# Local-attention stack: scores over four row groups into four PSUM banks shared with the outputs, and a new step order

## The chip, the core and the metric

The kernel runs on one core of a Trainium2 chip as one program. The metric is device time in microseconds (us), the median of several executions. One execution was also taken with the hardware profiler; its trace gives start and duration of every instruction on the five engines: TensorE (PE, with its weight loads as PEld), VectorE (DVE), ScalarE (ACT), GpSimd (POOL) and SyncE (SP, which here only issues DMAs).

## The reference, cut to what matters

The input is 16 sequences of 256 tokens with 128 features, in float32. A first part applies one small attention block, one mixture-of-experts block and one retention block. After it comes the stack that the change is about, six layers deep:

```python
for i in range(DEPTH):                                   # DEPTH = 6
    x = attn_layer(shift_tokens(x), ...) + x             # 16 heads of 64, window 32
    x = ffn_layer(shift_tokens(x), ...) + x

# attn_layer, per sequence and head:
q, k = rotary(l2norm(q) * qs), rotary(l2norm(k) * ksc)   # rotary with position-dependent scale
sim  = einsum("bhwie,bhwje->bhwij", q_windows, k_two_windows) * 8   # 32 queries against 64 keys
out  = einsum("bhwij,bhwje->bhwie", softmax(where(mask, -max, sim)), v_two_windows)
return out @ Wo

# ffn_layer: LayerNorm, x @ W1 + b1, a * gelu(gate), @ W2 + b2   (inner width 341)
```

So in the stack each window of 32 queries sees 64 keys: its own window and the one before. All arithmetic is float32.

## The kernel before, in words

**Units.** The stack is cut into 96 units: one sequence in one layer (`Unit`, 6 layers of 16). Two sequences share a feed-forward (`Forward`, 48 of them). A unit is a list of small steps, each a method that issues a few instructions on one engine:

- `pqk.G.k` (PE, four matmul instructions of 128x256) projects queries (k=0) or keys (k=1) of head group G into one of two PSUM banks. Four heads of a group lie on the four groups of 32 partitions. `sq` (ACT) squares the result, `t2` and `rot` (DVE) multiply it with the rotary tables, `add.G` (POOL) adds the two. The PSUM bank is free when `sq`, `t2` and `rot` are done.
- `nr.0` and `nr.1` (PE) sum the squares per head, `rnA`, `rnB`, `rnC` (DVE, ACT, DVE) make the reciprocal norm, `bcD` (SP) writes it to DRAM and reads it back spread over partitions (one DMA `ndr<-rn`, then eight `bc<-ndr`), and `norm.G` (POOL) multiplies it in.
- `s` (PE) computes scores. A float32 matmul is two weight loads and two matmul instructions; one `s` step holds 32 matmuls of 32x32 weights against 64 columns, so 64 matmul instructions. There are eight `s` steps in a unit. `sm` (DVE) adds the mask while it copies the scores out of PSUM; `mx`, `sub`, `exp`, `su`, `rec`, `nm` (DVE, POOL, ACT, DVE, DVE, DVE) make the softmax.
- `pv.i` (PE) projects the values, `vc.i` (ACT) copies them to SBUF, and `vs.0`, `vs.1` (SP, four DMAs `v<-v` each) make a copy that is shifted by one window.
- `pt`, `pTc` (PE, ACT) transpose the probabilities, `o.hu.tt` (PE, 64 matmul instructions, four steps in a unit) computes outputs, which read both copies of the values; `oTc` (ACT) copies them out of PSUM, `y.0`, `y.1` and `xsu` (PE, PE, DVE) project and add to x.
- A feed-forward is `fn`, `nat`, `st`, `rs`, `z`, `trf`, `fz` (LayerNorm with two transposes), then `fg`, `gl`, `fa`, `fh` three times, `fy` and `xsf`.

**PSUM.** Eight banks: two for `pqk`, two that all small results (`misc`) take in turn, two for scores (`ps_sc`) and two for outputs (`ps_ob`). A score tile is [128, 2, 512], for half the row groups (`hu` = 0 or 1), and an output tile is [128, 2, 512] for half the tokens (`tt`); each of the two pools has one buffer, so tiles of a pool follow each other in it.

**Order.** Nothing is scheduled at run time or by the framework: every engine executes its instructions in the order in which the steps are written. That order is the string `ORDER` (215 words, one iteration handles two units). In iteration j a word such as `s.0.0.1:2` calls step `s(0, 0, 1)` of unit 2j+2, `fy:-4` that of unit 2j-4; iterations overlap, so one iteration works on units that are up to nine apart. `:2` in one iteration is `:0` in the next. `BRIDGE` is the same for the passage from the first part. SP too takes its DMAs in this order: one that has to wait holds up those behind it. Weights of the next layer are issued by `follow` when the last unit has used the old ones.

Of the kernel before, what the change touches and what calls it, by code (L numbers as in the profile page):

```python
# [15 lines left out]
P = 128  # L16
# [94 lines left out]
def kernel(ctx: ExitStack, tc: tile.TileContext, a: dict, widths: dict, out: bass.AP):  # L111
# [742 lines left out]
    ps_o = ctx.enter_context(tc.tile_pool(name="ps_ob", bufs=1, **psum))  # L854
# [35 lines left out]
    def load_ff(l):  # L890
        w1 = kc.tile([P, 2 * FF], F32, tag="w1", name=f"w1_{l}")
        w2 = kc.tile([P, 3, D], F32, tag="w2", name=f"w2_{l}")
        nc.sync.dma_start(out=w1, in_=a["w1"][l])
        nc.sync.dma_start(out=w2[:, 0:2, :], in_=a["w2"][l, 0:256].rearrange("(c p) n -> p c n", p=P))
        nc.sync.dma_start(out=w2[0 : FF - 256, 2, :], in_=a["w2"][l, 256:FF])
        return w1, w2
# [3 lines left out]
    class Unit:  # L900
# [118 lines left out]
        def p_s(self, hu):  # L1019
            return self.tile(ps_s, [P, 2, 2, 2, 2, 2 * WIN], "s", hu, tag="s")  # L1020

        def s(self, hu, tt, gh):
            ps, qk = self.p_s(hu), self.qk_t
            for G in (2 * gh, 2 * gh + 1):
                for hf in range(2):
                    for b in range(4):
                        for r2 in range(2):
                            rows = slice(32 * (2 * hu + r2), 32 * (2 * hu + r2) + 32)
                            at = WIN * (4 * tt + b)
                            keys = qk[G][rows, 1, hf, at : at + 2 * WIN]  # L1030
                            if b % 2 == 0:
                                keys = keys.rearrange("f (n t) -> f n t", n=2)[:, ::-1, :]
                            nc.tensor.matmul(  # L1033
                                ps[32 * b : 32 * b + 32, r2, tt, G // 2, G % 2, :],
                                lhsT=qk[G][rows, 0, hf, WIN + at : 2 * WIN + at],
                                rhs=keys,
                                start=(hf == 0),
                                stop=(hf == 1),
                            )
# [8 lines left out]
        def sm(self, hu):  # L1048
            nc.vector.tensor_tensor(  # L1049
                self.t_sm(hu).rearrange("n r t g p c -> n r (t g p c)"),  # L1050
                self.p_s(hu).rearrange("n r t g p c -> n r (t g p c)"),
# [40 lines left out]
        def t_pT(self, hu, tt):  # L1092
            return self.tile(s3, [P, 512], "pT", hu, tt, bufs=3)
# [5 lines left out]
        def p_o(self, tt):  # L1099
            return self.tile(ps_o, [P, 2, 4, P], "o", tt, tag="o")  # L1100
# [349 lines left out]
```

## Time and profile before

| | |
|---|---|
| median of 3 executions | 4274.9 us (4269.47 to 4275.85) |
| profiled execution, its own time | 4277.4 us |
| its span, first to last instruction | 4275.7 us |
| mean granted TensorE clock | 0.969 of full speed |
| PE busy | 4036.9 us (94%) |
| DVE busy | 2940.5 us (69%) |
| POOL busy | 2527.3 us (59%) |
| ACT busy | 2077.0 us (49%) |

A line of the trace names the source line, engine, operation, tiles (out<-in), shape, count and time. L1033 is the matmul of `s`, L1111 that of `o`, L921 `pqk`, L955 `nr`, L1015 the DMAs of `vs`, L980 and L986 those of `bcD`, L1239 `fy`. In "idle before" or in the waits, the name behind the arrow is what the engine waited for. A busy PE is not PE at its peak: ends of matmuls are modelled, and a wait can hide under the last matmul's modelled end.

### The profile page before, as it was taken

Reading aid. Unit: us, or ns where it says so; the run is one execution under the profiler, and the core shown is the slowest. Engines: PE = TensorE matmul, PEld = TensorE weight load, DVE = VectorE, ACT = ScalarE, POOL = GpSimd, SP = SyncE. Lnnn points to the kernel's source line nnn. Section 1 sums busy time; section 2 is a strip of 40 time slices with the busy share of each in tenths; the row PEclk is TensorE's granted clock in tenths of the full one; section 3 lists DMA queues with packets and bytes.
Section 4 is the critical chain, followed back from the end, with each engine's and each line's share of the span. In section 5 each row is a group of like instructions: output and inputs, shape, how many; then the busy total and the mean of one; then the engine's idle time right before and its main releaser. Section 6 shows DMA issues by size and latency. Waiting matters only on the chain.

```text
span 4275.7 us, 216376 instructions
## 1 busy us (share of the span) xinstructions
PE 4036.9 (94%) x100320; PEld 2776.4 (65%) x100320; DVE 2940.5 (69%) x5436; ACT 2077.0 (49%) x3344; POOL 2527.3 (59%) x1419
## 2 busy tenths in 40 slices
PE   6999978999999999999999999999999999999998
PEld 4666655666666666666666666666666666666664
DVE  4677646677777677667777766767677777667774
ACT  2555534455554445444554544545445544545453
POOL 2454556666665666656666665666556666656661
PEclk8999988999999999999999999999999999999999
DMA  3111112222222222222222222122232212222231
GB/s 98 44 41 48 36 40 67 69 60 65 70 58 53 69 65 60 70 64 57 65 58 70 60 68 71 48 63 64 65 72 57 68 44 71 63 69 67 48 74 44
DMA packets 209187, 260.84 MB, mean 61 GB/s; under 512 B 54174, under 2 KB 164892, under 8 KB 207388
## 3 DMA queue, kind: packets, MB, share of 16 engines
q1 hardware_dynamic: 207852, 246.74, 23.2%
q8 instruction: 786, 12.88, 1.3%
q14 instruction: 117, 0.96, 0.1%
q10 hardware_dynamic: 432, 0.26, 0.0%
HBM read 140.98 MB, written 17.83 MB: 37 GB/s over the span
## 4 chain that ended last, share of the span: by engine, by line
PE 68%; DMA 9%; DVE 8%; POOL 6%; ACT 4%; issue 3%; SPq 3%; POOLq 0%; ACTq 0%; DVEq 0%
PE pqk L921 13%; PE s L1033 10%; PE o L1111 9%; PE pv L999 7%; DMA v<-v 6%; PE y L1130 5%; PE nr L955 4%; PE fy L1239 3%; PE pt L1088 3%; POOL qk L993 3%; PE fg L1209 2%; PE fa L1222 2%; PE p L330 2%; DVE sm L1082 1%; SPq L986 1%
## 5 line engine op out<-in xcount | busy, mean ns | idle before, releaser
L946 POOL TENSOR_TENSOR qk<-qk,t 128x1024 f32<-128x1024 f32 x384 | 906.6, 2363 | 282.1 <-DVE qk L940 276.0
L993 POOL TENSOR_TENSOR qk<-qk,bc 128x1024 f32<-128x1024 f32 x384 | 947.4, 2484 | 79.9 <-DMA v<-v 73.0
L1064 POOL TENSOR_TENSOR sm<-sm,mx 128x1024 f32<-128x1024 f32 x192 | 365.9, 1906 | 991.0 <-DVE mx L1060 274.3
L921 PE MATMUL pqk<-xs,wqk 128*128 128x256 f32 x3072 | 852.9, 406 | 20.0 <-ACT sq L929 9.6
L1033 PEld LDWEIGHTS s<-qk 32*32 32x32 f32 x49152 | 536.6, 104 | 393.6 <-issue 376.3
L929 ACT ACTIVATE sq<-pqk 128x512 f32<-128x512 f32 x768 | 454.2, 599 | 665.1 <-DVE qk L940 355.5
L940 DVE TENSOR_TENSOR qk<-pqk,rot 128x512 f32<-128x512 f32 x768 | 515.1, 681 | 308.4 <-PE pqk L921 249.2
L935 DVE TENSOR_TENSOR t<-pqk,rot 128x512 f32<-128x512 f32 x768 | 521.3, 685 | 287.3 <-ACT sq L929 140.3
L1033 PE MATMUL s<-qk 32*32 32x64 f32 x49152 | 665.9, 223 | 16.0 <-issue 10.3
L921 PEld LDWEIGHTS pqk<-xs,wqk 128*128 128x128 f32 x3072 | 547.1, 194 | 144.2 <-issue 50.9
L1111 PEld LDWEIGHTS o<-pT,v 64*64 64x64 f32 x24576 | 427.5, 140 | 310.9 <-issue 160.3
L1111 PE MATMUL o<-pT,v 64*64 64x32 f32 x24576 | 480.0, 225 | 94.8 <-DMA v<-v 91.8
L1096 ACT COPY pT<-pt 128x512 f32<-128x512 f32 x384 | 224.4, 584 | 471.4 <-PE pt L1088 236.8
L999 PE MATMUL pv<-wv,xs 128*64 128x512 f32 x1536 | 419.8, 626 | 4.6 <-DMA wv<-in_wv_dram 4.6
L1082 DVE TENSOR_TENSOR sm<-sm,rec 128x1024 f32<-128x1024 f32 x192 | 401.3, 2090 | 0.0
L1130 PE MATMUL y<-oT,wo 128*128 128x256 f32 x1536 | 383.8, 393 | 1.4 <-issue 1.1
L1049 DVE TENSOR_TENSOR sm<-s,c_band 128x1024 f32<-128x1024 f32 x192 | 233.9, 1218 | 145.2 <-PE s L1033 144.2
L1130 PEld LDWEIGHTS y<-oT,wo 128*128 128x128 f32 x1536 | 280.4, 192 | 44.6 <-issue 1.3
L1123 ACT COPY oT<-o 128x512 f32<-128x512 f32 x384 | 216.3, 589 | 161.7 <-PE o L1111 161.7
L1008 ACT COPY v<-pv 128x512 f32<-128x512 f32 x384 | 224.4, 585 | 122.8 <-PE pv L999 117.6
L1072 DVE TENSOR_REDUCE su<-sm 128x16 f32<-128x1024 f32 x192 | 232.4, 1210 | 40.6 <-ACT sm L1068 40.5
L1088 PE MATMUL pt<-ident,sm 128*128 128x128 f32 x1536 | 247.1, 284 | 1.8 <-issue 1.0
(189 smaller groups left out, 4976.9 us busy)
## 6 DMA issues: line engine op xcount, KB each, us to landing
bc<-ndr SPq DMA_DIRECT2D x768, 128.0 KB
v<-v SPq DMA_DIRECT2D x576, 128.0 KB
v<-v SPq DMA_DIRECT2D x192, 64.0 KB
rot_l<-in_rot_dram SPq DMA_DIRECT2D x12, 512.0 KB
rot<-rot_l SPq DMA_DIRECT2D x12, 512.0 KB
wqk<-in_wqk_dram SPq DMA_DIRECT2D x24, 256.0 KB
rot<-rot SPq DMA_DIRECT2D x6, 1024.0 KB
ndr<-rn SPq DMA_DIRECT2D x96, 32.0 KB
```

What stands on the lines that cost most here:

```text
L921: nc.tensor.matmul(self.p_qk(G, k)[:, hf, :], lhsT=weights["qk", G, self.l][:, k, hf, :], rhs=xq, start=True, stop=True)
L929: nc.scalar.activation(self.squares(G)[:, k], self.p_qk(G, k), AF.Square)
L935: nc.vector.tensor_tensor(self.t_2(G)[:, k], self.p_qk(G, k)[:, ::-1, :], weights["rot", self.l][:, 1, k], ALU.mult)
L940: nc.vector.tensor_tensor(self.qk_t[G][:, k, :, WIN : WIN + T], self.p_qk(G, k), weights["rot", self.l][:, 0, k], ALU.mult)
L946: nc.gpsimd.tensor_tensor(to, to, self.t_2(G), ALU.add)
L993: nc.gpsimd.tensor_tensor(to, to, self.bcast()[:, G, :, None, :].to_broadcast([P, 2, 2, T]), ALU.mult)
L999: nc.tensor.matmul(self.misc("pv", i)[64 * p : 64 * p + 64, :], lhsT=xs[self.g][:, self.seq, cols], rhs=weights["v", self.l][:, p, :], sta ...
L1033: nc.tensor.matmul(ps[32 * b : 32 * b + 32, r2, tt, G // 2, G % 2, :], lhsT=qk[G][rows, 0, hf, WIN + at : 2 * WIN + at], rhs=keys, start=( ...
L1082: nc.vector.tensor_tensor(s3, s3, self.t_rec(hu)[:, :, None].to_broadcast([P, 16, 2 * WIN]), ALU.mult)
L1088: nc.tensor.transpose(pt[:, j * P : (j + 1) * P], sm[:, j // 2, tt, j % 2].rearrange("n p c -> n (p c)"), ident)
L1111: nc.tensor.matmul(o[64 * e : 64 * e + 64, p, 2 * hu + m, WIN * b : WIN * b + WIN], lhsT=vals[self.u % 2][rows, 1 - b % 2, 2 * tt + b // 2 ...
L1130: nc.tensor.matmul(self.misc("y")[:, 0:T], lhsT=weights["o", self.l][:, ch, :], rhs=self.t_oT()[:, ch, :], start=(ch == 0), stop=(ch == 7),)
```

## The change

1. A score tile now holds all four row groups, [128, 4, 512], in four banks. A step `s.tt.G` takes one head group and both halves `hf`, and its innermost loop goes over the four row groups (before: two head groups, two row groups). There are still eight `s` steps of 32 matmuls.
2. The output tile is [128, 2, 2, 512] and takes the same four banks: `ps_sc` with one buffer and one tag, "so", for both. Scores of a unit, outputs of the unit before, scores of the next unit follow each other in it. `sm.0` and `sm.1` each read two of the four banks.
3. `z`, the LayerNorm's scaling in the stack, goes from DVE (subtract, multiply) to ACT (Identity with bias and scale); for it `rs` gets two more small POOL instructions. `ln_z` has one buffer instead of two, `pT` four instead of three.
4. The load of W1 and W2 is split: W1 is issued when the last `fg`/`fa` has used the old one, W2 as before after `fy`.
5. `ORDER` and `BRIDGE` are replaced by new ones of the same length. Both orders of the stack are shown; of `BRIDGE` only that it changes.

```diff
@@ -851,7 +851,6 @@
     s2 = ctx.enter_context(tc.tile_pool(name="s2", bufs=2, **right))
     ps_qk = ctx.enter_context(tc.tile_pool(name="ps_qk", bufs=2, **psum))
     ps_s = ctx.enter_context(tc.tile_pool(name="ps_sc", bufs=1, **psum))
-    ps_o = ctx.enter_context(tc.tile_pool(name="ps_ob", bufs=1, **psum))
 
 
     ring = []
@@ -887,13 +886,16 @@
         nc.sync.dma_start(out=w, in_=a["wo2"][l].rearrange("p (c n) -> p c n", c=8))
         return w
 
-    def load_ff(l):
+    def load_w1(l):
         w1 = kc.tile([P, 2 * FF], F32, tag="w1", name=f"w1_{l}")
+        nc.sync.dma_start(out=w1, in_=a["w1"][l])
+        return w1
+
+    def load_w2(l):
         w2 = kc.tile([P, 3, D], F32, tag="w2", name=f"w2_{l}")
-        nc.sync.dma_start(out=w1, in_=a["w1"][l])
         nc.sync.dma_start(out=w2[:, 0:2, :], in_=a["w2"][l, 0:256].rearrange("(c p) n -> p c n", p=P))
         nc.sync.dma_start(out=w2[0 : FF - 256, 2, :], in_=a["w2"][l, 256:FF])
-        return w1, w2
+        return w2
 
 
 
@@ -1016,27 +1018,26 @@
 
 
 
-        def p_s(self, hu):
-            return self.tile(ps_s, [P, 2, 2, 2, 2, 2 * WIN], "s", hu, tag="s")
-
-        def s(self, hu, tt, gh):
-            ps, qk = self.p_s(hu), self.qk_t
-            for G in (2 * gh, 2 * gh + 1):
-                for hf in range(2):
-                    for b in range(4):
-                        for r2 in range(2):
-                            rows = slice(32 * (2 * hu + r2), 32 * (2 * hu + r2) + 32)
-                            at = WIN * (4 * tt + b)
-                            keys = qk[G][rows, 1, hf, at : at + 2 * WIN]
-                            if b % 2 == 0:
-                                keys = keys.rearrange("f (n t) -> f n t", n=2)[:, ::-1, :]
-                            nc.tensor.matmul(
-                                ps[32 * b : 32 * b + 32, r2, tt, G // 2, G % 2, :],
-                                lhsT=qk[G][rows, 0, hf, WIN + at : 2 * WIN + at],
-                                rhs=keys,
-                                start=(hf == 0),
-                                stop=(hf == 1),
-                            )
+        def p_s(self):
+            return self.tile(ps_s, [P, 4, 2, 2, 2, 2 * WIN], "s", tag="so")
+
+        def s(self, tt, G):
+            ps, qk = self.p_s(), self.qk_t[G]
+            for hf in range(2):
+                for b in range(4):
+                    for r in range(4):
+                        rows = slice(32 * r, 32 * r + 32)
+                        at = WIN * (4 * tt + b)
+                        keys = qk[rows, 1, hf, at : at + 2 * WIN]
+                        if b % 2 == 0:
+                            keys = keys.rearrange("f (n t) -> f n t", n=2)[:, ::-1, :]
+                        nc.tensor.matmul(
+                            ps[32 * b : 32 * b + 32, r, tt, G // 2, G % 2, :],
+                            lhsT=qk[rows, 0, hf, WIN + at : 2 * WIN + at],
+                            rhs=keys,
+                            start=(hf == 0),
+                            stop=(hf == 1),
+                        )
 
 
         def t_sm(self, hu):
@@ -1048,7 +1049,7 @@
         def sm(self, hu):
             nc.vector.tensor_tensor(
                 self.t_sm(hu).rearrange("n r t g p c -> n r (t g p c)"),
-                self.p_s(hu).rearrange("n r t g p c -> n r (t g p c)"),
+                self.p_s()[:, 2 * hu : 2 * hu + 2].rearrange("n r t g p c -> n r (t g p c)"),
                 band[:, None, :].to_broadcast([P, 2, 512]),
                 ALU.add,
             )
@@ -1090,14 +1091,14 @@
                 )
 
         def t_pT(self, hu, tt):
-            return self.tile(s3, [P, 512], "pT", hu, tt, bufs=3)
+            return self.tile(s3, [P, 512], "pT", hu, tt, bufs=4)
 
         def pTc(self, hu, tt):
             nc.scalar.copy(self.t_pT(hu, tt), self.misc("pt", hu, tt))
 
 
         def p_o(self, tt):
-            return self.tile(ps_o, [P, 2, 4, P], "o", tt, tag="o")
+            return self.tile(ps_s, [P, 2, 2, 4, P], "o", tag="so")[:, tt]
 
         def o(self, hu, tt):
             o, pT = self.p_o(tt), self.t_pT(hu, tt)
@@ -1172,17 +1173,20 @@
         def rs(self):
             rs = self.tile(s3, [P, 4], "rs")
             nc.gpsimd.tensor_tensor(rs, rs, mhalf[:, 0:4], ALU.pow)
+            nb, mv = self.tile(s3, [P, 4], "nb"), self.tile(s3, [P, 4, 2], "ln_mv")
+            nc.gpsimd.tensor_tensor(nb, mv[:, :, 0], rs, ALU.mult)
+            nc.gpsimd.tensor_scalar(nb, nb, -1.0, None, ALU.mult)
             if self.last:
                 nc.sync.dma_start(out=self.tile(s3, [P, 4, D], "f_res", bufs=2), in_=kept[self.g])
 
         def t_z(self):
-            return self.tile(s3, [P, 4, D], "ln_z")
+            return self.tile(s3, [P, 4, D], "ln_z", bufs=1)
 
         def z(self):
-            nat, mv, rs = self.t_nat(), self.tile(s3, [P, 4, 2], "ln_mv"), self.tile(s3, [P, 4], "rs")
+            nat, rs, nb = self.t_nat(), self.tile(s3, [P, 4], "rs"), self.tile(s3, [P, 4], "nb")
             for k in range(4):
-                nc.vector.tensor_scalar(
-                    self.t_z()[:, k, :], nat[:, k, :], mv[:, k, 0:1], rs[:, k : k + 1], ALU.subtract, ALU.mult
+                nc.scalar.activation(
+                    self.t_z()[:, k, :], nat[:, k, :], AF.Identity, bias=nb[:, k : k + 1], scale=rs[:, k : k + 1]
                 )
 
         def trf(self):
@@ -1205,7 +1209,7 @@
 
         def fg(self, n):
             f0, m = FFC[n]
-            w1 = weights["ff", self.l][0]
+            w1 = weights["w1", self.l]
             nc.tensor.matmul(
                 self.misc("fg", n)[0:m, :], lhsT=w1[:, FF + f0 : FF + f0 + m], rhs=self.t_zT(), start=True, stop=True
             )
@@ -1218,7 +1222,7 @@
 
         def fa(self, n):
             f0, m = FFC[n]
-            w1 = weights["ff", self.l][0]
+            w1 = weights["w1", self.l]
             nc.tensor.matmul(
                 self.misc("fa", n)[0:m, :], lhsT=w1[:, f0 : f0 + m], rhs=self.t_zT(), start=True, stop=True
             )
@@ -1238,7 +1242,7 @@
             for n, (_, m) in enumerate(FFC):
                 nc.tensor.matmul(
                     self.misc("fy"),
-                    lhsT=weights["ff", self.l][1][0:m, n, :],
+                    lhsT=weights["w2", self.l][0:m, n, :],
                     rhs=self.t_h()[0:m, n, :],
                     start=(n == 0),
                     stop=(n == 2),
@@ -1269,50 +1273,51 @@
 
 
     ORDER = """
-        add.1:3 o.0.0:0 sq.1.0:3 pqk.3.1:3 vs.1:0 fn:-2 rot.0.1:3 norm.1:2 pTc.1.1:0 t2.0.1:3 rot.3.1:3 sm.1:1
-        sq.0.1:3 nat:-2 o.1.0:0 norm.0:2 rec.0:1 pqk.3.0:3 t2.3.0:3 oTc.0.1:0 pv.2:1 oTc.0.0:0 t2.3.1:3 o.0.1:0
-        rot.3.0:3 pv.0:1 sq.3.1:3 s.0.0.0:2 add.0:3 sq.3.0:3 nm.0:1 mx.1:1 st:-2 vc.2:1 pqk.2.1:3 pv.3:1 sq.2.1:3
-        o.1.1:0 pqk.2.0:3 vc.3:1 norm.3:2 sq.2.0:3 sub.1:1 norm.2:2 s.0.1.0:2 vc.0:1 t2.2.1:3 rot.2.1:3 pqk.1.0:4
-        pv.1:1 exp.1:1 nr.0:3 t2.2.0:3 nr.1:3 rs:-2 vc.1:1 su.1:1 rot.2.0:3 rec.1:1 rnA:3 rnB:3 pt.0.0:1 rnC:3 z:-2
-        pqk.1.1:4 s.0.0.1:2 trf:-2 pTc.0.0:1 pt.0.1:1 s.0.1.1:2 fz:-2 pTc.0.1:1 nm.1:1 fy:-4 sm.0:2 oTc.1.0:0 bcD:3
-        s.1.0.0:2 add.3:3 fg.0:-2 gl.0:-2 xsf:-4 t2.1.0:4 sq.1.1:4 s.1.1.0:2 t2.1.1:4 rot.1.0:4 mx.0:2 pt.1.1:1 pv.0:2
-        pTc.1.1:1 vs.0:1 oTc.1.1:0 add.2:3 vc.0:2 s.1.0.1:2 rot.1.1:4 pt.1.0:1 y.0:0 sq.1.0:4 s.1.1.1:2 sub.0:2
-        pqk.0.1:4 exp.0:2 norm.0:3 norm.1:3 pqk.0.0:4 sm.1:2 rot.0.1:4 o.0.0:1 sq.0.1:4 t2.0.1:4 add.1:4 su.0:2 y.1:0
-        rec.0:2 xsu:0 pTc.1.0:1 mx.1:2 o.1.0:1 pv.3:2 t2.0.0:4 oTc.0.1:1 sub.1:2 pqk.3.1:4 nm.0:2 s.0.0.0:3 fa.0:-2
-        oTc.0.0:1 rot.0.0:4 fh.0:-2 vc.3:2 sq.3.1:4 fg.1:-2 sq.0.0:4 exp.1:2 vs.1:1 o.0.1:1 fa.1:-2 o.1.1:1 rot.3.1:4
-        pqk.3.0:4 gl.1:-2 t2.3.1:4 su.1:2 sq.3.0:4 norm.2:3 pqk.2.1:4 oTc.1.1:1 s.0.1.0:3 norm.3:3 rec.1:2 add.0:4
-        fh.1:-2 pt.0.0:2 pTc.0.0:2 fg.2:-2 oTc.1.0:1 t2.3.0:4 s.0.1.1:3 pt.0.1:2 t2.2.1:4 rot.3.0:4 rot.2.1:4
-        pqk.2.0:4 s.0.0.1:3 gl.2:-2 nm.1:2 pTc.0.1:2 sq.2.1:4 sq.2.0:4 sm.0:3 t2.2.0:4 rot.2.0:4 pv.1:2 vc.1:2 nr.0:4
-        mx.0:3 add.3:4 pqk.1.1:5 nr.1:4 rnA:4 pqk.0.0:5 s.1.1.0:3 t2.1.1:5 rnB:4 fa.2:-2 rnC:4 pv.2:2 bcD:4 sq.0.0:5
-        sub.0:3 fh.2:-2 s.1.0.0:3 y.0:1 rot.1.1:5 sq.1.1:5 pqk.1.0:5 add.2:4 s.1.0.1:3 rot.0.0:5 t2.0.0:5 y.1:1
-        exp.0:3 t2.1.0:5 vs.0:2 rot.1.0:5 vc.2:2 s.1.1.1:3 su.0:3 pt.1.0:2 pqk.0.1:5 xsu:1 pt.1.1:2 pTc.1.0:2
+        bcD:2 fa.2:-4 gl.2:-4 rot.0.0:3 exp.1:1 o.0.0:0 su.1:1 pqk.1.1:3 add.0:3 o.1.1:0 t2.3.0:3 sq.1.1:3 sub.0:1
+        pv.2:1 o.1.0:0 sq.3.0:3 t2.1.1:3 fh.2:-4 norm.2:2 rot.3.0:3 oTc.1.1:0 fy:-4 oTc.0.1:0 norm.3:2 norm.0:2
+        rec.1:1 oTc.1.0:0 oTc.0.0:0 exp.0:1 nm.1:1 s.1.2:2 rot.1.1:3 vc.2:1 xsf:-4 pqk.1.0:3 pv.0:1 s.0.2:2 vc.0:1
+        sq.1.0:3 pt.1.0:1 norm.1:2 pqk.3.1:3 fn:-2 t2.3.1:3 pTc.1.0:1 rot.1.0:3 s.0.3:2 su.0:1 y.0:0 s.0.1:2 y.1:0
+        nat:-2 s.1.1:2 t2.1.0:3 add.1:3 rot.3.1:3 add.3:3 pqk.2.1:3 s.0.0:2 sq.3.1:3 pqk.2.0:3 sq.2.1:3 rec.0:1 st:-2
+        pv.1:1 s.1.0:2 xsu:0 nm.0:1 sq.2.0:3 pt.0.1:1 rot.2.1:3 vc.1:1 pt.0.0:1 vs.0:1 s.1.3:2 pTc.0.1:1 pt.1.1:1
+        pTc.0.0:1 rot.2.0:3 pTc.1.1:1 t2.2.1:3 pv.1:2 nr.0:3 t2.2.0:3 sm.1:2 vs.1:1 sm.0:2 vc.1:2 nr.1:3 rnA:3 rnB:3
+        rnC:3 pqk.0.0:4 t2.0.0:4 pqk.0.1:4 add.2:3 pv.3:2 t2.0.1:4 mx.1:2 o.0.0:1 pv.2:2 sq.0.0:4 rs:-2 bcD:3 mx.0:2
+        rot.0.0:4 sq.0.1:4 z:-2 rot.0.1:4 vc.3:2 sub.1:2 o.0.1:1 pqk.1.1:4 vc.2:2 trf:-2 pqk.2.1:4 t2.1.1:4 rot.1.1:4
+        exp.1:2 vs.1:2 sub.0:2 o.1.1:1 sq.1.1:4 add.0:4 fz:-2 t2.2.1:4 rot.2.1:4 pqk.2.0:4 oTc.1.0:1 oTc.1.1:1 pv.0:2
+        t2.2.0:4 exp.0:2 su.1:2 o.1.0:1 su.0:2 fg.0:-2 rec.0:2 sq.2.1:4 norm.3:3 oTc.0.1:1 norm.1:3 pqk.1.0:4
+        oTc.0.0:1 rot.2.0:4 vc.0:2 norm.2:3 nm.0:2 rot.1.0:4 rec.1:2 s.0.3:3 y.0:1 t2.1.0:4 gl.0:-2 nm.1:2 sq.2.0:4
+        s.1.1:3 pqk.3.1:4 s.1.3:3 y.1:1 xsu:1 sq.1.0:4 s.0.1:3 s.1.2:3 fa.0:-2 fg.1:-2 fh.0:-2 add.1:4 s.0.2:3
+        pqk.3.0:4 gl.1:-2 rot.3.1:4 sq.3.1:4 pt.1.0:2 pt.1.1:2 norm.0:3 sq.3.0:4 t2.3.1:4 pTc.1.1:2 s.0.0:3 pTc.1.0:2
+        pqk.0.1:5 rot.3.0:4 pt.0.0:2 s.1.0:3 add.2:4 pTc.0.0:2 sm.0:3 t2.3.0:4 pt.0.1:2 sm.1:3 vs.0:2 pTc.0.1:2 pv.3:3
+        nr.0:4 nr.1:4 rnA:4 vc.3:3 rnB:4 rot.0.1:5 rnC:4 pqk.0.0:5 fa.1:-2 t2.0.1:5 sq.0.0:5 mx.1:3 add.3:4 o.0.1:2
+        sub.1:3 fg.2:-2 t2.0.0:5 sq.0.1:5 pqk.3.0:5 fh.1:-2 mx.0:3
     """.split()
 
 
     BRIDGE = """
...
     """.split()
 
     weights = {}
@@ -1338,8 +1343,13 @@
             weights["v", l + 1] = load_v(l + 1)
         elif method == "y" and q == NSEQ - 1 and count[key] == 2:
             weights["o", l + 1] = load_o(l + 1)
+        elif method in ("fg", "fa") and q == NSEQ - 2:
+            both = (l, "w1")
+            count[both] = count.get(both, 0) + 1
+            if count[both] == 6:
+                weights["w1", l + 1] = load_w1(l + 1)
         elif method == "fy" and q == NSEQ - 2:
-            weights["ff", l + 1] = load_ff(l + 1)
+            weights["w2", l + 1] = load_w2(l + 1)
 
     issued = set()
     with tc.manual_schedule():
@@ -1371,7 +1381,8 @@
     with tc.manual_schedule():
         weights["v", 0] = load_v(0)
         weights["o", 0] = load_o(0)
-        weights["ff", 0] = load_ff(0)
+        weights["w1", 0] = load_w1(0)
+        weights["w2", 0] = load_w2(0)
         for j in range(-3, len(units) // 2 + 3):
             for method, args, d in parse(ORDER):
                 u = 2 * j + d
```

## The prediction

> **What bounds the kernel now.** I read the page first, for the busy shares and the chain that ended last.
>
> ```profile
> PE 4036.9 (94%) x100320; PEld 2776.4 (65%) x100320; DVE 2940.5 (69%) x5436; ACT 2077.0 (49%) x3344; POOL 2527.3 (59%) x1419
> PE 68%; DMA 9%; DVE 8%; POOL 6%; ACT 4%; issue 3%; SPq 3%; POOLq 0%; ACTq 0%; DVEq 0%
> ```
>
> PE is the bound, but a tenth of the chain is DMA. Next, busy time by stretch: the steady part of the stack, and in it the instructions of `fy`, six per iteration.
>
> ```profile
> 864.00:4165.00 3301.00, 3199.20 (x87022) 2189.39 (x87024) 2347.08 (x3436) 1643.33 (x2509) 2061.78 (x924) 0.98 0.26 63
> 864.00:4165.00 3301.00, 124.96 (x264) 46.41 (x263) 0.98 0.26 63
> ```
>
> 264/6 is 44 iterations, so one takes 3301/44 = 75.0 us. What PE does in it, and what it waits for, is in the timeline of PE, that of SP, and the waits:
>
> ```profile
> 2553.27 0.66 PE L1088 MATMUL pt<-ident,sm 128*128 128x128 f32 x4
> 2553.76 1.03 PE L921 MATMUL pqk<-xs,wqk 128*128 128x256 f32 x4
> 2554.63 0.60 PE L1088 MATMUL pt<-ident,sm 128*128 128x128 f32 x4
> 2555.67 0.30 PE L1111 MATMUL o<-pT,v 64*64 64x32 f32 x2 [0.44 <-DMA v<-v]
> 2556.46 1.27 PE L1111 MATMUL o<-pT,v 64*64 64x32 f32 x62 [0.49 <-DMA v<-v]
> 2557.66 1.13 PE L921 MATMUL pqk<-xs,wqk 128*128 128x256 f32 x4
> ```
>
> ```profile
> 2543.81 0.38 SPq L980 DMA_DIRECT2D ndr<-rn  x1
> 2546.16 4.60 SPq L986 DMA_DIRECT2D bc<-ndr  x8
> 2550.86 5.60 SPq L1015 DMA_DIRECT2D v<-v  x8
> ```
>
> ```profile
> PEld o L1111 <- DMA v<-v: 112.9, 119, 4.2
> PE o L1111 <- DMA v<-v: 91.8, 100, 3.8
> ```
>
> Steps follow each other with no gap (start to start: `pt` 0.49, `pqk` 0.87) until `o.0.0:0` meets values that are not there: their DMAs stand in SP's queue behind the nine of `bcD`. The two wait rows add to 204.7 us, 4.3 us for each of 48 iterations.
>
> **The PE work in one iteration.** Read as start-to-next-start in the timeline, a step has one length where the next step uses the array in the same shape, and a longer one where the shape changes: `pqk` 0.87 or 1.06, `pt`, `fn` and `trf` 0.49 or 0.53, `nr` 0.90 or 1.03, `y` 1.83 or 1.92, `fa` 0.96 or 1.05, `fg` 0.86 or 0.95, `fy` 2.77, `pv` 1.01, `o` 1.07, `s` 0.79. Both orders have the same 73 PE steps: 16 `pqk`, 16 `s`, 8 each of `o`, `pv`, `pt`, 4 `nr`, 4 `y`, 3 `fa`, 3 `fg`, and `fn`, `trf`, `fy`. By their neighbours the old order sums to 70.8 us; 75.0 - 70.8 = 4.2 us are waits, about the 4.3 of the values.
>
> The new order has three more `pqk` and two more `fg` before a step of their own shape, one more `nr` followed by its like, and one pair of adjacent `s` (the second taken at 0.53, its 0.79 less the 0.26 in which the first half starts, below); two `pt` and one `y` lose it. With the same lengths it sums to 69.8: **-1.0 us** an iteration, certain as far as neighbours go.
>
> **The `s` step.** A cut of PE's timeline through one step shows 32 of its 64 matmul instructions starting in the first 0.25 us; the whole is
>
> ```profile
> 2503.61 0.45 PE L1033 MATMUL s<-qk 32*32 32x64 f32 x32
> 2503.61 0.85 PE L1033 MATMUL s<-qk 32*32 32x64 f32 x64
> ```
>
> (first row: window ending at 2503.86). The last of the 64 starts 0.64 after the first and the next step 0.14 later. The first 32 go at 8 ns each, the rest at 12 ns, on the same eight tiles of the array. So in the second half something other than occupied tiles sets the pace, and sixteen tiles would not change that. Bounds: 0 (all pace is supply of instructions) to 0.40 us (both halves at twice the first half's rate: 0.25 + 0.14 = 0.39 a step). With only the second half at the rate of the first it is 0.64, a gain of 0.15. A loss I exclude by the nearest rows: in the first part L282 cycles over four row groups and L330 over two, with 1024 instructions of the same shapes, and PE is busy 89.0 us for L282, 149.7 for L330. I take 0.02, near the lower end because the slow half is the shape at hand and L282 has 128 to 256 columns: 16 x 0.02 = **-0.3 us**.
>
> The Trainium skill ("TensorE: Matmul & The Clock Gate", Part 3, Measured speedup vs the span model) says that tiles at different positions start about 4 ns apart and that sixteen of them gave 10.6 times the speed of one. By it, as an estimate, a step would be 64 x 4 ns + 0.14 = 0.40 us and the kernel near 3800; the 12 ns of the slow half speak against it.
>
> **The waits.** I go through the places where PE could now wait.
>
> *Values.* In the old order PE has 12.9 us of steps from the end of `nr.1:4` to `o.0.0:0` (`pqk`, `s`, `fa`, `pv`, `s`, `y`, `pqk`, `s`, `y`, `s`, `pt`, `pqk`, `pt`), against 1.0 for `rnA`, `rnB` and `rnC`, 2.35 to the first `bc`, 4.7 for `bc` and 5.6 for `v`: 13.7. In the new order `vs.0:1` stands before the next `bcD`, SP has been idle, and from the end of `pv.1:1` PE has 9.0 us (`s`, `pt`, `pt`, `s`, `pt`, `pv`, `nr`, `nr`, `pqk`, `pqk`, `pv`) to `o.0.0:1`; needed are 0.6 of waiting for ACT, 0.6 for `vc` and 5.6. Spare 2.2. The even unit's `vs` still stand behind `bcD:3`, but its `o.0.1:2` comes over 20 us later. I take this wait as gone, with 0.3 left.
>
> *Turns of the four banks.* Each unit adds a wait for `sm` before `o` and one for `oTc` before `s`; behind the waiting step all of PE is queued. `s.1.3:2` to `o.0.0:1` has 6.4 us of PE steps, `s.1.0:3` to `o.0.1:2` 5.4, against two `sm` at 1.22 and DVE's `t2` steps ahead of them, up to 1.4: 3.9. `o.1.0:0` to `s.1.2:2` has `fy`, 2.8, `o.1.0:1` to `s.0.3:3` has `fg` and `pqk`, 1.9, against two `oTc` at 0.59 plus 0.1. Spare 0.6 at the least. Cost 0, and 0.2 taken for late ACT work (`exp.0:2` stands ahead of those `oTc`).
>
> The skill ("TensorEngine Tiling (Array Packing)", PSUM Bottleneck) warns that tiling speeds up TensorE but not the copy out of PSUM. It speaks against this change exactly at these turns; the sum would then be that of the third rival.
>
> *DVE after `nr.1:4`.* From there DVE has a solid block: `rnA`, `rot`, `rnC`, `t2`, `mx`, `t2`, then `fh.1`, which `fa.2` waits for, `mx.0`, `rot.0.0`. By their rows 0.21 + 0.68 + 0.55 + 0.69 + 1.21 + 0.69 + 0.75 = 4.8 us, against 4.7 of PE steps: late by 0.1 to 0.4. Then on POOL `add.0:3` 2.36, `sub.0:1` 1.91, `norm.2:2` 2.48 before `s.1.2:2`: DVE 6.7 + POOL 6.75 = 13.5 against 13.8 of PE steps. Cost 0.7 with what slips, 0 to 1.5.
>
> Sum of waits 1.2 us; 0.3 if all cover holds, 4.2 if as much is lost as now.
>
> **At no cost.** `z`: four of 0.47 us leave DVE, four of 0.48 (the first part's `z_m`) join ACT, two of 0.20 and 0.24 join POOL; `trf` comes over 2 us after them, and ACT is half idle; if exposed, 2.4 us. W1 and W2: five layer ends, W1 has 40 us to its `fg`. One buffer less for `ln_z`: its reader is half an iteration old. The bridge and the tail (302 and 111 us by stretch) I leave at 0, within 15 us.
>
> **Sum.** 69.8 - 0.3 + 1.2 = 70.7 us an iteration, 4.3 less than 75.0; 46 iterations' worth (44 steady, and half the weight for the four at the ends) is 198 us. From the profiled execution's own 4277.4 that gives 4079; the median lies 2.5 lower: **4077 us**. Bounds of this case: 69.8 + 0.3 - 2.4 (`s` at 0.64) = 67.7 gives 3940; 69.8 + 4.2 = 74.0 gives 4229.
>
> **Rivals.**
> 1. *Sixteen tiles pay.* For: L282 against L330. Against: the slow second half. Steps at 0.39: 16 x 0.40 = 6.4 us an iteration instead of 0.3, 280 us more: about 3800. From 0.64 down this rival decides. 0.10.
> 2. *Waits only move.* PE again waits some 4 to 5 us, for values (their DMAs took 5.6 us here, and would need 7.8) or in DVE's block: 74 to 74.8 an iteration, 4230 to 4266. For: three covers have under 0.6 us to spare, and DMA and clock vary. 0.11. If the new order changes nothing at all, about 4275: 0.03.
> 3. *The turns are not hidden* (slower). One tile with one buffer: `o` waits for two `sm` (2.44), `s` for two `oTc` (1.18), twice an iteration, 7.3 us if fully exposed: 69.8 - 0.3 + 1.2 + 7.3 = 78.0, +138 us: 4413. It decides from 4.3 us of the 7.3 on. For: two `oTc` have 0.6 us to spare, DVE is busy 69% and strictly in order. Against: 5.4 to 6.4 us of PE work before `o`. 0.16.
>
> **How the numbers follow.** The forecast has 0.60. Differences within 0.2% (8.5 us) could not be told from none here. Faster: 0.60 + 0.10 + 0.11 = 0.81; same 0.03; slower 0.16. The range leaves out the third rival and the lower part of the first: 3930 to 4260.
>
> **What would show it.** Right: `o`'s waits for DMA v fall from 205 us to under 40; an iteration at 70 to 71.5; an `s` step still near 0.77; DVE `ln_z` rows gone from DVE. Wrong: `s` steps below 0.6 (first rival); rows "o <- DVE sm" or "s <- ACT oT" of over 100 us on PE (third); `v<-v` still the first releaser of `o`, or `fa` waiting for `fh` by more than 1.5 us an iteration (second).

## The result, and the profile after

The changed kernel took 4201.2 us in the median (4198.15 to 4201.93) against 4275.4 for the kernel before on the same chip: a ratio of 0.9824, 95% interval 0.9807 to 0.9841. That is 74 us, or 1.8%, faster. The prediction was 198 us faster (4077): the sign was right and the time lies in the range, but nearly two thirds of the forecast gain are missing.

The page's busy shares and the chain that ended last, after:

```profile
PE 3950.9 (94%) x100320; PEld 2720.3 (65%) x100320; DVE 2862.0 (68%) x5244; ACT 2150.6 (51%) x3535; POOL 2634.3 (63%) x1515
PE 69%; DVE 9%; ACT 7%; DMA 5%; POOL 4%; issue 3%; SPq 2%; ACTq 0%; POOLq 0%; DVEq 0%
```

DMA's part of the chain fell from 9% to 5%, but DVE and ACT took more of it. `fy` by stretch, over the same 38 steady iterations (228/6) of each kernel, before first, then after:

```profile
863.80:3712.00 2848.20, 108.09 (x228) 40.25 (x228) 0.98 0.26 63
```

```profile
850.50:3602.40 2751.90, 108.11 (x229) 40.29 (x229) 1.00 0.28 65
```

An iteration went from 2848.2/38 = 74.95 to 2751.9/38 = 72.42 us, where 70.7 was forecast (the last of the 229 begins the next iteration). The waits, of PE and PEld, after:

```profile
PEld s L1034 <- POOL qk L995: 102.4, 92, 6.0
PE s L1034 <- POOL qk L995: 50.8, 44, 5.2
PE fy L1243 <- DVE f_h L1232: 26.1, 35, 0.9
PE o L1112 <- DMA v<-v: 1.9, 3, 1.0
```

The wait of `o` for the values, 91.8 us on PE and 112.9 on PEld before, is gone (1.9 and 2.3 after). In its place `s` waits for POOL's `norm` (0.8 us on PE's row before) and `fy` for DVE's `f_h`.

The two rows of `o` before can't be added, though. PEld (TensorE's weight loads) and PE (its matmuls) idle there at the same time, and their waits end at the same instant. At the place whose PE rows the prediction shows (0.44 and 0.49 us of waiting), PEld has

```profile
2555.67 0.19 PEld L1111 LDWEIGHTS o<-pT,v 64*64 64x64 f32 x2 [0.68 <-DMA v<-v]
2556.46 1.16 PEld L1111 LDWEIGHTS o<-pT,v 64*64 64x64 f32 x62 [0.60 <-DMA v<-v]
```

Counted once, the two rows cover 113.0 us of the run, 2.4 for each of 48 iterations, not 204.7 and 4.3.

**The clock.** A second cost went with this wait. In the 38 iterations before, TensorE's granted clock was half of full speed in 21 stretches of 3.4 to 10.2 us, 102 us together. Each of them begins between 0.4 us before and 3.0 us after the start of an `o.0.0`, the step that waits for values twice in an iteration (`o.0.0:0` and `o.0.0:1`). The first row below shows PE's busy time in one such stretch and, behind it, the granted clock, 0.50; the others are an `o` step inside it and one right behind it:

```profile
2637.90:2644.70 6.80, 6.80 (x78) 0.50 0.00 0
2639.36 1.94 PE L1111 MATMUL o<-pT,v 64*64 64x32 f32 x64
2644.95 1.14 PE L1111 MATMUL o<-pT,v 64*64 64x32 f32 x64
```

After the change one stretch of 3.4 us is left in the 38 iterations. Against the same steps outside of such stretches, the steps in them took 1.0 us an iteration more before the change, 1.5 if those at which the wait itself stands are counted too, and less than 0.1 after. With the prediction's step lengths, an iteration before was 70.8 us of steps, 1.0 to 1.5 of slow clock and 2.7 to 3.2 of waits; after, it is 69.8 of steps and 2.6 of waits. So of the 2.5 us saved, 1.0 to 1.5 are the clock and 1.0 the steps. The waits as a whole shrank by 0.1 to 0.6 only: others took the place of the values'.

Last, PE's timeline through one `s` step, first the window ending 0.19 us after its start, then the whole:

```profile
2518.01 0.39 PE L1034 MATMUL s<-qk 32*32 32x64 f32 x32
```

```profile
2518.01 0.85 PE L1034 MATMUL s<-qk 32*32 32x64 f32 x64
```

Half of the instructions start within 0.19 us instead of 0.25, but the whole step is 0.85 as it was, and the next step still begins 0.78 us after its start.

**Where the 75.7 us of the profiled executions (4277.4 to 4201.7) come from.** The 38 steady iterations gave 96.3. The stretch up to the first `fy` became 13.3 shorter (863.8 to 850.5), the one from the end of the 38 iterations to PE's last instruction 33.9 longer (559.7 to 593.5). Some 15 us of these two are work that only changed sides: counted at the prediction's step lengths, PE has 198 us of stack steps before the first `fy` in the old order and 183 in the new, and 493 against 508 behind the 38th. So the start neither gained nor lost (1.5 us), and the end, which should have gained about 4 us in each of its iterations, lost 19. Behind the 38th iteration 55 us ran at half clock, before the change 37; at the 0.4 to 0.55 us that each such microsecond cost in the steady part (1.0 to 1.5 for 2.7 us an iteration), that is an estimated 6 to 9 of the 19.

### The profile page after: what moved, and what is told of

Same layout as the page of the kernel before. It is cut to its first block, busy times and chain, and to the rows that moved or that the text cites. A ratio compares the mean times of both kernels' runs of the same rounds, so it can differ in the third digit from the quotient of the medians.

```text
span 4199.9 us, 216259 instructions
## 1 busy us (share of the span) xinstructions
PE 3950.9 (94%) x100320; PEld 2720.3 (65%) x100320; DVE 2862.0 (68%) x5244; ACT 2150.6 (51%) x3535; POOL 2634.3 (63%) x1515
## 4 chain that ended last, share of the span: by engine, by line
PE 69%; DVE 9%; ACT 7%; DMA 5%; POOL 4%; issue 3%; SPq 2%; ACTq 0%; POOLq 0%; DVEq 0%
PE s L1034 14%; PE pqk L923 12%; PE y L1131 9%; PE pv L1001 7%; PE pt L1089 5%; PE nr L957 5%; PE o L1112 3%; POOL qk L995 3%; PE fy L1243 3%; DMA v<-v 2%; DVE t L937 2%; PE fg L1213 2%; PE fa L1226 2%; SPq L988 2%; PE p L330 2%
## 5 line engine op out<-in xcount | busy, mean ns | idle before, releaser
L948 POOL TENSOR_TENSOR qk<-qk,t 128x1024 f32<-128x1024 f32 x384 | 936.5, 2444 | 602.7 <-DVE t L937 554.8
L995 POOL TENSOR_TENSOR qk<-qk,bc 128x1024 f32<-128x1024 f32 x384 | 997.4, 2624 | 194.9 <-DMA v<-v 123.0
L1034 PEld LDWEIGHTS s<-qk 32*32 32x32 f32 x49152 | 506.5, 103 | 390.6 <-issue 261.0
L1034 PE MATMUL s<-qk 32*32 32x64 f32 x49152 | 654.1, 226 | 62.8 <-POOL qk L995 50.8
L923 PEld LDWEIGHTS pqk<-xs,wqk 128*128 128x128 f32 x3072 | 537.7, 191 | 164.5 <-issue 63.1
L1112 PEld LDWEIGHTS o<-pT,v 64*64 64x64 f32 x24576 | 399.4, 135 | 273.2 <-issue 157.1
L1112 PE MATMUL o<-pT,v 64*64 64x32 f32 x24576 | 444.4, 221 | 12.7 <-issue 8.9
L1083 DVE TENSOR_TENSOR sm<-sm,rec 128x1024 f32<-128x1024 f32 x192 | 436.2, 2272 | 2.4
L1219 ACT ACTIVATE f_gl<-fg,vecs 128x512 f32<-128x512 f32 x144 | 98.8, 686 | 339.8 <-PE fg L1213 325.6
L957 PEld LDWEIGHTS nr<-sq,c_band 128*32 128x32 f32 x12288 | 182.1, 111 | 89.8 <-ACT pT L1097 76.3
```

The costliest lines, as they stand in the source:

```text
L923: nc.tensor.matmul(self.p_qk(G, k)[:, hf, :], lhsT=weights["qk", G, self.l][:, k, hf, :], rhs=xq, start=True, stop=True)
L948: nc.gpsimd.tensor_tensor(to, to, self.t_2(G), ALU.add)
L957: nc.tensor.matmul(nr[32 * G : 32 * G + 32, :], lhsT=gather[:, b, :], rhs=self.squares(G)[:, :, hf, WIN * b : WIN * b + WIN], start=(b == ...
L995: nc.gpsimd.tensor_tensor(to, to, self.bcast()[:, G, :, None, :].to_broadcast([P, 2, 2, T]), ALU.mult)
L1034: nc.tensor.matmul(ps[32 * b : 32 * b + 32, r, tt, G // 2, G % 2, :], lhsT=qk[rows, 0, hf, WIN + at : 2 * WIN + at], rhs=keys, start=(hf = ...
L1083: nc.vector.tensor_tensor(s3, s3, self.t_rec(hu)[:, :, None].to_broadcast([P, 16, 2 * WIN]), ALU.mult)
```

## The experiments

The runs form four groups, each on one chip: e1 to e4; c0, e5, e8 and e9; e7, e10, c1 and e13; e14. The kernel before, run beside each group, took 4253, 4251, 4246 and 4247 us. Ratios are to the kernel before in the same group, and it is ratios that are compared between groups. c0, the changed kernel again, is the control. "Iteration" is the mean of the 38 steady ones in the run's trace.

| run | base and edit | median us | ratio (95% interval) | iteration us |
|---|---|---|---|---|
| c0_after_again | changed kernel | 4175.2 | 0.9832 (0.9807 to 0.9857) | 72.09 |
| e1_two_rows | changed, `s` over two row groups | 4190.6 | 0.9860 (0.9834 to 0.9885) | 72.33 |
| e9_half_columns | changed, `s` with 32 columns | 4122.7 | 0.9704 (0.9681 to 0.9727) | 71.08 |
| e7_z_on_dve | changed, `z` on DVE | 4233.8 | 0.9966 (0.9946 to 0.9986) | 73.63 |
| e3_h_early | changed, `fh.2` earlier | 4170.6 | 0.9803 (0.9775 to 0.9831) | 71.65 |
| e4_vs_late | changed, `vs.1:2` later | 4177.5 | 0.9814 (0.9789 to 0.9839) | 72.13 |
| e5_transpose_late | changed, `xsf` later | 4166.3 | 0.9808 (0.9782 to 0.9834) | 72.11 |
| c1_three_moves | changed, e3 + e4 + e5 | 4150.5 | 0.9769 (0.9744 to 0.9795) | 71.59 |
| e14_s_later | c1, `s.1.2:2` later | 4140.1 | 0.9745 (0.9719 to 0.9771) | 71.62 |
| e10_z_alone | before, `z` on ACT | 4228.6 | 0.9961 (0.9942 to 0.9981) | 74.29 |
| e2_values_first | before, values' DMAs first | 4178.8 | 0.9835 (0.9812 to 0.9859) | 73.07 |
| e8_values_and_z | before, e2 + e10 | 4125.6 | 0.9708 (0.9686 to 0.9731) | 71.79 |
| e13_stats_later | e8, `st` later | 4105.5 | 0.9675 (0.9650 to 0.9700) | 71.34 |

### Are the sixteen tiles worth anything?

```diff
-            for hf in range(2):
+            for rh in range(2):
+              for hf in range(2):
                 for b in range(4):
-                    for r in range(4):
+                    for r in (2 * rh, 2 * rh + 1):
```

> Changed kernel, with the 64 matmul instructions of an `s` step issued over two row groups at a time (8 tiles in turn, as before the change) and all else kept. Theory: from the 33rd instruction on the supply of instructions sets the pace (0.265 us to the 33rd start in both kernels), so the sixteen tiles were worth nothing: an `s` step stays at 0.78 to 0.79 us and the time within 0.2% of the changed kernel's 4201 (4193 to 4210). Rival: the sixteen tiles are worth the 0.058 us by which their first half starts sooner (0.180 against 0.238), 16 times in 48 iterations: 45 us slower, 4246.

> The changed kernel itself, as a control on the chip of the other runs. It should stand to the kernel before as it did (0.981 to 0.984), and to the kernel with two row groups at a time (0.986, 0.983 to 0.989) within 0.2% if the supply of instructions sets the pace of `s`, 1.0% below it if sixteen tiles are worth the 45 us.

The two intervals overlap, so the medians (0.3% apart) do not tell the kernels apart at this size, though the 1.0% of the rival would show. The traces tell more: without the stretches at half clock (27 us in e1's 38 iterations, 3 in the control's) an iteration takes about 72.0 us in both. I took the starts of the 64 matmul instructions of `s` in some 480 steps of each run (medians, us after the first start):

```
                                 17th    33rd    64th    next step
before (8 tiles in turn)         0.136   0.266   0.641   0.785
changed (16 tiles in turn)       0.093   0.265   0.640   0.784
e1_two_rows (8 tiles)            0.136   0.265   0.640   0.785
e9_half_columns (16 tiles)       0.079   0.238   0.562   0.683
```

With sixteen tiles the first 32 instructions start sooner and then the 33rd waits until 0.265, the time at which it started with eight. From there everything is equal. The gain of the tiling is 0.001 us a step.

> Changed kernel, with the scores of only 32 of the 64 keys computed: every matmul of an `s` step has 32 columns instead of 64, their number is the same, and `sm` reads the 32 twice. It leaves out half of the scores. Theory (supply of instructions): the 64 starts come as before (33rd at 0.265, last at 0.64 us) and only the last stream is shorter: the step stays at 0.70 to 0.79 us, the time within 60 us of the changed kernel's. Rival (occupied tiles or the stream of columns sets the pace of the second half): the second half takes half as long, the step falls to 0.55 or less, 16 x 0.2 x 48 = 150 us or more less.

```diff
+                        keys = keys[:, 0] if b % 2 == 0 else keys[:, 0:WIN]
                         nc.tensor.matmul(
-                            ps[32 * b : 32 * b + 32, r, tt, G // 2, G % 2, :],
+                            ps[32 * b : 32 * b + 32, r, tt, G // 2, G % 2, 0:WIN],
```

One `s` step in PE's timeline of that run:

```profile
2518.76 0.75 PE L1035 MATMUL s<-qk 32*32 32x32 f32 x64
```

Half the columns take 0.10 us, 13%, off a step. Its 0.683 us lie just below the theory's 0.70 to 0.79 and far from the rival's 0.55. But the starts did not come "as before": the 64th moved from 0.640 to 0.562, so the columns have some part in the pace. An iteration is 1.0 us shorter, the run some 54 us (0.9704 against 0.9832). Carried on to no columns at all, 0.78 - 2 x 0.10 = 0.58 us would be left. If that estimate from two points holds, most of the step goes by the number of instructions, which sixteen tiles do not change. What in their supply sets the pace was not taken apart.

### Was the gain the values' wait, and did it need the new order?

```diff
-  vc.1:1 su.1:1 ...   pTc.1.1:1 vs.0:1 ...   exp.1:2 vs.1:1 ...   vc.1:2 nr.0:4 ...   exp.0:3 t2.1.0:5 vs.0:2
+  vc.1:1 vs.0:1 vs.1:1 su.1:1 ...            vc.1:2 vs.0:2 nr.0:4 ...
```

> Kernel before the change, with only the values' DMAs moved in the order: vs.0:1 and vs.1:1 right behind vc.1:1, vs.0:2 right behind vc.1:2, so that on SP they stand ahead of the nine DMAs of bcD. Theory: the wait of `o` for the values is all that there was to gain, and it needed neither the four banks nor a new order: the 205 us of these rows go, `bc` lands 4 to 6 us later, which `norm` hides, and the time is 4080 to 4130. Rival: the wait turns into one of `norm` for `bc` and of `s` for `norm`, as it did in part in the changed kernel (2.6 us of 4.3 an iteration came back): about 4200. Second rival: the wait is not made by SP's queue, and the time stays within 0.5% of 4275.

Three words moved in the old order give 0.9835, the result of the whole change (0.9832). But the theory expected 4080 to 4130. It counted the two rows of `o` as 205 us, where they cover 113, and here too part of the gain came back. Of the 1.9 us by which an iteration is shorter than before the change (74.95 to 73.07), 0.6 to 1.1 are the clock: 28 us at half clock are left of 102, none of them beginning at an `o.0.0`. In e10 below, where the wait for values stays, 89 us stay. So the slow clock goes with this wait; why, no run here shows. The row `o <- DMA v` is gone from PE's waits, and two others stand there:

```profile
PE pqk L921 <- DVE qk L940: 34.6, 36, 2.7
PE trf L1190 <- DVE ln_z L1184: 32.5, 43, 4.2
```

The second was 10.1 us before. So what came back here is mostly not `norm`, the rival, but DVE: behind the values' wait stood DVE's lateness, hidden by it. That led to `z`, the one part of the change that takes work from DVE.

> Kernel before, with the values' DMAs ahead of bcD as in e2_values_first, and of the change's parts only the move of `z` from DVE to ACT (with `nb` on POOL). In e2_values_first an iteration took 72.2 us, with 0.64 us of waiting of `trf` for ln_z and 0.45 of `pqk` for DVE. Theory: with the wait for the values gone DVE is what is late, and `z` off DVE takes both away: about 0.8 to 1.2 us an iteration, 40 to 55 us less than e2_values_first (4179), 4124 to 4139, better than the whole change without its tiling and its order. Rival: ACT is late with `z` in turn, or another DVE step takes the place: within 0.3% of 4179.

> Kernel before, with only the move of `z` from DVE to ACT (`nb` on POOL), and the values' DMAs where they were. With the values moved as well, this part was worth 53 us (4179 to 4126). Theory: alone it is worth little, since whatever time PE gains ahead of o.0.0:0 it waits there for the values, whose DMAs start and land when they did: 0 to 12 us, 4239 to 4252 where the kernel before has 4251 to 4253. Rival: DVE's lateness is paid beside the values' wait, not inside it, and the 53 us come in full: about 4200.

> Changed kernel, with `z` back on DVE (no `nb`). Theory: in the new order too DVE's block after nr.1 is near the limit (fy waits 0.9 us for f_h in each iteration), so four instructions of about 0.47 us put back on DVE make trf late, as they did in the old order with the values first: 0.5 to 1.2 us an iteration, 25 to 55 us slower than the changed kernel's 4175, 4200 to 4230. Rival: in the new order there is room for them on DVE: within 0.3% of 4175.

The edit is the change's own for `z` and `rs` (or its reverse), nothing else. The theory holds in all three in direction, with e10 and e7 just past its ranges (and the 72.2 us that the first of these expectations gives for e2 is below the table's mean, 73.07). With the values first, `z` on ACT is worth 1.3% (0.9835 to 0.9708), and the row of `trf` waiting for `ln_z` on PE falls to 5.3 us. With the values where they were it is worth 0.4%, some 17 us: more than the 12 expected at most, a third of the 53. In the new order, taking it back costs 1.3% (0.9832 to 0.9966), some 57 us. PE's waits of e7_z_on_dve:

```profile
PE trf L1191 <- DVE ln_z L1185: 33.2, 47, 4.2
PE fy L1240 <- DVE f_h L1229: 31.5, 43, 0.9
```

So the new order and the sixteen tiles without `z` are only 0.3% faster than the kernel before, and values and `z` in the old order, with neither, beat the whole change by 1.3%.

### What does PE wait for in the new order?

```diff
 e3:  -  su.1:1 ... t2.1.1:3 fh.2:-4 norm.2:2            +  fh.2:-4 su.1:1 ... t2.1.1:3 norm.2:2
 e4:  -  exp.1:2 vs.1:2 sub.0:2 ... vs.0:2 pTc.0.1:2     +  exp.1:2 sub.0:2 ... vs.0:2 vs.1:2 pTc.0.1:2
 e5:  -  vc.2:1 xsf:-4 pqk.1.0:3 ... sq.1.0:3 pt.1.0:1   +  vc.2:1 pqk.1.0:3 ... sq.1.0:3 xsf:-4 pt.1.0:1
 e14: -  nm.1:1 s.1.2:2 rot.1.1:3 ... pv.0:1 s.0.2:2     +  nm.1:1 rot.1.1:3 ... pv.0:1 s.1.2:2 s.0.2:2
```

> Changed kernel, with the product `fh.2:-4` (DVE) moved ahead of su.1:1 in the order, about 5 us of DVE work sooner. Theory: the 0.9 us that `fy` waits for DVE f_h is paid in each of 48 iterations because fh.2 stands too late on DVE: the row goes to under 10 us (26 on `fy` itself, and the wait of its weight loads beside it) and the time falls by 30 to 45 us, to 4156 to 4171. Rival: the DVE work behind it (sub, add, su) is then late by as much, norm.2:2 on POOL follows it, and s.1.2:2 waits instead: within 0.3% of 4201.

An iteration became 0.44 us shorter than in the control (72.09 to 71.65). From `o.1.0:0` to `fy` the mean excess over the shortest seen fell from 0.95 to 0.24 us, and the excess from `fy` to the step behind s.1.2:2 rose by about 0.3: theory and rival each in part. The medians (0.9803 against 0.9832) do not tell the run from the control, and two traces of the changed kernel itself are 0.33 us apart (72.42 and 72.09); the two places in the order are what shows it.

> Changed kernel, with vs.1:2 (eight DMAs of values, wanted only over 10 us later) moved from behind bcD:3 to behind the next vs.0:2. Theory: the eight DMAs of `bc` take 7 to 9 us from first issue to the start of `norm`, not the 4.7 of the prediction, because those of the values run right behind them; without these `bc` lands 1 to 2 us sooner, s.0.3:3 and s.1.1:3 no longer wait about 1 us an iteration for norm, and the time falls by 25 to 50 us, to 4150 to 4176. Rival: `bc` lands when it did (what is late is its own issue or POOL's work ahead of norm.3:3): within 0.3% of 4201.

The theory misses. The medians agree with the control, an iteration is 72.13 against 72.09, and most of POOL's idle time ahead of `norm` still stands, all of it now named `bc` (in the control 85.6 us are put down to `v<-v` and 74.1 to `bc`, together 159.7):

```profile
POOL qk L995 <- DMA bc<-ndr: 138.3, 86, 6.9
```

The values' DMAs behind `bc` are at most a small part of what makes `bc` late. SP's timeline and POOL's in the changed kernel:

```profile
2579.18 4.67 SPq L988 DMA_DIRECT2D bc<-ndr  x8
```

```profile
2587.78 5.66 POOL L995 TENSOR_TENSOR qk<-qk,bc 128x1024 f32<-128x1024 f32 x2 [1.25 <-DMA bc<-ndr]
```

4.67 us is the time in which SP issues the eight DMAs; `norm` starts 8.6 us after the first of them. No v DMA follows these eight for another 23 us. For the iteration's other unit, where eight follow at once, it is 9.3 us.

> Changed kernel, with xsf:-4 (in the last layer the transposes `tr_e` that wait for DVE `end`) moved two PE steps later in the order, to just before pt.1.0:1. Theory: in the last layer the new order puts `tr_e` only one `s` step behind `fy`, so PE waits 13.8 us in 8 places; all of it goes, and the last layer's iterations become 1.5 to 2 us shorter: 10 to 18 us, 4183 to 4191 where the changed kernel has 4201. Rival: DVE `end` is late because of DVE's own order, not of PE's, and PE meets the same wait two steps later: no change beyond 0.2%.

The wait of `tr_e` for DVE `end` falls from 13.6 us in the control to 3.2, less than all of it. The median is 9 us lower (0.9808 against 0.9832), in the direction and just under the size expected, and inside what the two intervals allow for no difference.

> Changed kernel with the three moves of e3_h_early, e4_vs_late and e5_transpose_late together. Alone they gave -5, +2 and -9 us against the changed kernel on the same chip (4175). Theory: fh earlier turned 0.7 us of the wait of fy into 0.35 us of a wait of s.1.2:2 for norm.2:2, tr_e's wait went; together 10 to 25 us, 4150 to 4165, still behind e8_values_and_z (4126). Rival: the waits removed come back elsewhere on PE: 4170 to 4178.

0.9769 against 0.9832: 27 us, just over the 10 to 25 expected. Of the profiles' difference (4173.2 to 4140.4 in span) 19 us lie in the 38 iterations and 16 behind them.

> c1_three_moves with s.1.2:2 moved two PE steps later, behind pqk.1.0:3 and pv.0:1 (2 us of PE work), so that norm.2:2 has time. In c1 an iteration still waits 0.51 us there, the largest that is left. Theory: POOL's chain (bc, add, sub, norm) is what the new order leaves PE waiting for, and a step placed 2 us later meets it done: 0.4 to 0.7 us an iteration, 15 to 30 us: 4121 to 4135, still over e13_stats_later (4105) because the ends of the stack stay. Rival: the wait moves to the next s (s.0.2:2 for norm.2 or s.0.3:2 for norm.3): within 0.3% of 4151.

The iteration did not move (71.59 and 71.62). The step now stands right before s.0.2:2, and the pair takes some 0.65 us more in the mean than at its shortest, where s.1.2:2 alone had 0.51. So the wait only moved on, as the rival said; the 10 us by which the median is lower are within the intervals. POOL sits idle ahead of `norm` until `bc` lands in both runs (132.6 and 150.9 us), so I take what PE meets to be the way from `nr` over `bc` to `norm`, for which a place two steps later is not far enough; no run here shortens that way.

### The fastest version

> e8_values_and_z (kernel before, values first, `z` on ACT) with st:-2 (nine small DVE instructions, about 2.2 us) moved from ahead of t2.2.1:3 and rot.2.1:3 to right behind them. In e8 pqk.1.0:4 waits 0.45 us an iteration for DVE's rot.2.1:3, whose buffer it takes. Theory: that wait goes, 15 to 25 us: 4100 to 4111. Rival: rs on POOL and z on ACT come later by 1.4 us and trf waits, or rot.2.0:3 is late in turn: within 0.3% of 4126.

```diff
-  nm.0:1 mx.1:1 st:-2 pqk.2.1:3 ... t2.2.1:3 rot.2.1:3 pqk.1.0:4
+  nm.0:1 mx.1:1 pqk.2.1:3 ... t2.2.1:3 rot.2.1:3 st:-2 pqk.1.0:4
```

As expected: 4105.5, and the row of `pqk` waiting for DVE's `rot` falls from 33.9 to 14.9 us:

```profile
PE pqk L921 <- DVE qk L940: 14.9, 11, 2.7
PE trf L1193 <- ACT ln_z L1187: 6.0, 3, 4.8
```

This is the old tiling and the old order with four words moved and `z` on ACT: 3.2% faster than the kernel before and 1.6% faster than the changed one.

## Why the prediction was right and wrong

- **Values.** Right that the wait goes, wrong in what it was worth. The 204.7 us count the same time twice, on PEld and on PE; once, it is 113.0, 2.4 us an iteration. That 4.3 came out "about" the 75.0 - 70.8 = 4.2 was luck: these 4.2 are 2.7 to 3.2 us of waits, not all for values, and 1.0 to 1.5 of half clock, for which the prediction has no term. The slow clock left with the wait, so the error in the reading did not show in the sum. The prediction's own working for the place, 13.7 us needed against 12.9 of cover, gave a wait of only 0.8.
- **Length of the steps.** Right: over 40 iterations of the changed kernel the shortest time seen at each place sums to 70.8 us, of which 0.92 is the wait of `fy` that was in every one: 69.9, against 69.8 worked out from the neighbours.
- **The `s` step.** Right in reading and near in size: 0.02 was taken, 0.001 measured. The first rival is dead. The Trainium skill ("TensorE: Matmul & The Clock Gate", Part 3, Measured speedup vs the span model) would have had, by an estimate from its 4 ns between tiles, 0.40 us for a step; measured are 0.784, and the measurement decides.
- **Turns of the banks.** Right: `o` waited 1.5 us in the whole run for `oT` (in two places), and no row of `o` for `sm` reaches PE's largest waits. The third rival, and with it the skill's warning of the copy out of PSUM ("TensorEngine Tiling (Array Packing)", PSUM Bottleneck), did not come about here.
- **The other waits: the main step that failed.** 1.2 us were taken, 72.4 - 69.8 = 2.6 were paid. Two terms make most of it. `fy` waits 0.9 us for `fh.2` in nearly every iteration; the prediction followed DVE's block up to `fa.2` and never on to `fy`, so this had no term at all. And `s` waits for `norm`, 0.5 us an iteration at s.0.3:3 and 0.1 to 0.15 at some others. For the way from `nr` over `bc` to `norm` there was no term either: the only length that the prediction gives `bc`, the 4.7 in its sum for the old order's values, is SP's time for issuing eight DMAs, not for their landing. The trace of before had the answer: its first `bc` was issued at 2546.16, and this row of POOL, the `norm` that reads it, is 9.5 us later.

```profile
2555.63 4.69 POOL L993 TENSOR_TENSOR qk<-qk,bc 128x1024 f32<-128x1024 f32 x2 [1.93 <-DMA v<-v]
```

  About 0.3 us more, at nr.1:3, carry the name "issue": the profile shows nothing that PE waited for. Over the 38 steady iterations 163 us (38 x 4.3) were forecast and 96 came: 67 of the missing 122.
- **The ends.** The bridge at 0 was right within 2 us (the new `BRIDGE` has 234 words, where the old one has 220). The tail was not: the forecast credited 46 iterations of saving, 38 of them steady, and so about 34 us behind these; measured is a loss of 19. That is 53 of the missing 122. Some 14 of it are `tr_e`, which waits for DVE `end` in the last layer because the new order puts it one `s` behind `fy`, and which no term covered. c1, nearly without it, still takes 30 us longer from the 38th iteration to the end than e8_values_and_z (562.3 against 531.8), of which 15 are the work that changed sides. Of the other 15 an estimated 8 to 11 go by the clock, at the same 0.4 to 0.55: 31 us of that stretch run at half clock in c1, 10 in e8. What brings the clock down there, perhaps waits of the last units, where PE has less other work beside `bc` and `norm`, was not tested.
- **`z` "at no cost".** Its cost was nil as said, but the label hid that the forecast hung on it: without `z` on ACT 1.3% of the 1.7% goes. The prediction priced what each part adds and not what it lets through.
- **Second rival** ("waits only move", 4230 to 4266). It named the mechanism, new waits in place of the old, and the wrong amount: 2.6 us an iteration, not 4 to 5. Its sign, `fa` waiting for `fh`, did not show; the wait was one step further on, at `fy`.

## What to carry to other kernels

When a change removes the largest wait, list what stands next behind it on every engine before crediting the gain: here DVE was late by over a microsecond an iteration right behind it (67 us in the two PE rows of e2), and with `z` on ACT in both, moving three DMA words and one DVE step in the old order did more than a new tiling with a new order. Count a wait once, on PE or on PEld, and look at the granted clock around it: here half clock cost another 1.0 to 1.5 us an iteration. Price a chain through DMAs from the first issue to the start of the reader, a row that the trace of before has, not from the time the queue spends on issuing. When the first half of a burst runs faster than the second, the second half's pace is the bound, and a change that quickens only the first is worth nothing.

## What the hardware showed that was not expected

- Sixteen tiles in turn bring the 17th instruction forward from 0.136 to 0.093 us and leave the 33rd where it was, 0.265; twice the tiles buy a head start that ends after 32 instructions.
- Halving the columns of those matmuls shortens a step only from 0.784 to 0.683 us.
- Waits of `o` for DMAs came with half the granted clock: all 21 slow stretches of the 38 iterations before, 102 us, begin at such a wait, and an `o` step in one of them takes 1.94 us instead of 1.14. With three words of the order moved, and the wait gone, 28 us were left.
- The name that a wait for DMAs carries can be wrong: POOL's `norm` reads `qk` and `bc` and no values, yet 85.6 of the 159.7 us that it waited in the control were put down to `v<-v`; with the eight of them that follow `bc` in each iteration moved away 138.3 us stood, all named `bc<-ndr`.
